# Mixing stage of a convolution and Laplace-operator kernel: a third output tile, weights one place sooner, POOL operations merged, sums evicted between the copies and run in pairs

## The chip, the cores and the metric

The kernel runs on one core of a Trainium2 chip. The metric is the device time of one execution in microseconds. A core has a matrix engine (PE, with its weight loads shown apart as PEld), a vector engine (DVE), an activation engine (ACT), a general engine (POOL), and a queue engine (SP) that here does nothing but issue DMAs. They work side by side and wait for each other through semaphores. PE writes its results into PSUM, eight banks per partition; ACT and DVE read them from there.

## The reference

Input is x of 16 images (b) with 16 channels and 256 x 256 points, fp32. There are two layers, each of the form x + layer(group-normalised x).

```python
# layer 0: circular 3x3 convolution
x = x + _L0_conv_ref(_gn(x), L0_conv_weight)
# layer 1: Laplace operator; alpha is the 2-D spectrum of gn(x)
alpha = jnp.fft.fft2(x, axes=(-2, -1))
A  = 1.0 / (omega1[:, None, None, None] - weights_pole1[None])
Bm = 1.0 / (omega2[:, None, None, None] - weights_pole2[None])
S  = jnp.einsum('ikpq,oikp,xikq->oxik', weights_residue, A, Bm)
output_residue1 = jnp.einsum('biox,oxik->bkox', alpha, S)
x1 = jnp.fft.ifft2(output_residue1, s=(Ny, Nx), axes=(-2, -1)).real
# residues, and exponentials exp(pole * t) of both directions
C = jnp.einsum('biox,oikp->bikpx', alpha, A)
D = jnp.einsum('bikpx,xikq->bikpq', C, Bm)
output_residue2 = jnp.einsum('bikpq,ikpq->bkpq', D, weights_residue)
E1 = jnp.exp(weights_pole1[..., None] * tyc)
E2 = jnp.exp(weights_pole2[..., None] * txc)
F  = jnp.einsum('kbpq,bipz->kbiqz', output_residue2, E1)
x2 = jnp.einsum('kbiqz,biqx->kizx', F, E2).real
x = x + (x1 + x2 / Nx / Ny)
```

What matters here are two lines: for every frequency (o, x) a 16 x 16 complex matrix `S` over channels (i, k) is formed, and the spectrum `alpha` of all images is multiplied by it (`output_residue1`). This is "mixing".

## The kernel before

The work runs in four stages, one after the other: the convolution with its norms (to about 600 us), the spectrum of the second layer (to about 1193 us), the mixing stage (to about 1863 us), and the inverse transform with the residue part and the output. In all but the mixing stage the change moves only a few loads and buffers.

The mixing stage is a loop over 32 *places* g, each of them four frequencies of one axis, and in each place over four *steps* n. A step does the following.

- `sums(n, w)`: 16 small matmuls (line 1032, two instructions each in the trace) multiply the weights `w` of the place by `ct` and so form a part of the matrices `S` of the next place g+1. They fill two banks `ps_s` out of a pool of four.
- `spread`: ACT (line 1049) and DVE (a stream shuffle, line 1052) copy these two banks into `sg` of the next place, twice each. Each engine begins with the other one's second bank: ACT reads bank 0 while DVE reads bank 1, and then they change over.
- `mix(m)`, four times: eight matmuls (line 1120, 16 instructions each in the trace) multiply `sg` of this place by the spectrum `abd` into a bank `ps_mix`, out of a pool of four. Each bank is then copied into the tile `yt` (line 1233), three by ACT and one by DVE, or two by each where ACT has other work in this step (`late`).
- `store`: four DMAs of 128 KB (line 1134) bring `yt` to the array `yD` in DRAM. `yt` has two buffers, one a step.
- `load`: up to four DMAs (line 1102 at n = 1, line 1107 at n = 2 and 3; nothing at n = 0) bring a part of the spectrum of the next place into `abd`.

All DMAs of stores and loads are issued on SP's queue, in the order of the program. Beside that run two generators, of which each step takes one piece. `weights(g + 2)` makes the weights that the sums of place g+1 use: three DVE operations at n = 0 (lines 903 to 910), a reciprocal and two more at n = 1 (lines 912 to 915), two at n = 2 (918 and 919), and then a POOL operation that spreads them into `w` (line 930; two buffers). `make_exps` makes the exponentials E1 and E2 in 16 rounds, of which each takes seven steps: POOL reduces the argument to the range of the sine (lines 1180 to 1195), ACT does Exp and Sin with a table load for each (1198 and 1201), POOL multiplies (1203 and 1205), and SP stores.

Nothing plans this order: `manual_schedule` keeps each engine's instructions in the order in which the program writes them, and each engine goes through its own in order. What a wait holds up is all that stands behind it on the same engine. Ahead of the loop `first_sums` makes the sums of the first place at once, and `finish_projections` (matmuls with `jmat`) finishes a part of the residues. At g = 30 and 31 `unmix_first` reads back, changes and writes again a part of the first place, on SP and DVE.

Of the kernel before, what the change touches and what calls it, by code (L numbers as in the profile page):

```python
# [9 lines left out]
FP = mybir.dt.float32  # L10
# [14 lines left out]
def conv_then_laplace_kernel(ctx: ExitStack, tc: tile.TileContext, a: dict, out: bass.AP):  # L25
# [28 lines left out]
    def const(name, shape):  # L54
        t = cp.tile(shape, FP, name=name, tag=name)
        later_loads.append((t, a[name]))
        return t

    cols = const("cols", [P, 24])
    kmask = const("kmask", [P, C])  # L60
    fold2 = const("fold2", [P, 2, 64])
    o2 = cp.tile([P, B, 2, 16], FP, name="o2", tag="o2")
    proj = cp.tile([P, 2, B, 16, 2], FP, name="proj", tag="proj")
    jmat = cp.tile([P, 3, P], FP, name="jmat", tag="jmat")
# [32 lines left out]
    tp = ptab.enter_context(tc.tile_pool(name="tables", bufs=1))  # L97
    vmr = tp.tile([P, 2, B, C], FP, name="vmr", tag="vmr")
# [59 lines left out]
    nc.sync.dma_start(out=jmat, in_=a["jmat"])  # L158
# [736 lines left out]
    def weights(g):  # L895
# [4 lines left out]
        u = up["u" if g else "u0"].tile([P, 4, 32, 4], FP, name="u", tag="u")  # L900
        w, den, e, f = (u[:, j] for j in range(4))
# [13 lines left out]
        nc.vector.scalar_tensor_tensor(f, w, nm0, pim, ALU.mult, ALU.add)  # L915
# [3 lines left out]
        nc.vector.tensor_tensor(v[:, :, 1], f, den, ALU.mult)  # L919
# [64 lines left out]
    yp = pool(p2, "yt", 2)  # L984
# [6 lines left out]
    zp = pool(p2, "between")  # L991
# [16 lines left out]
    zp.tile([P, 384], FP, name="between", tag="between")  # L1008
# [34 lines left out]
    def spread(n, *pairs):  # L1043


        for odd in range(2):
# [37 lines left out]

    def finish_projections():


        for ro in range(2):
            ps = pm.tile([P, B, 16], FP, name="ps_o", tag="ps_mix")
            nc.tensor.matmul(ps, lhsT=jmat[:, 0], rhs=accs[:, ro], start=True, stop=False)  # L1090
            nc.tensor.matmul(ps, lhsT=jmat[:, 2 - ro], rhs=accs[:, 1 - ro], start=False, stop=True)
            nc.vector.tensor_copy(o2[:, :, ro], ps)

# [67 lines left out]
    def make_exps(which):  # L1161
# [5 lines left out]
        nc.sync.dma_start(out=t, in_=a[("ty", "tx")[which]].to_broadcast([P, N]))  # L1167
        sign, phase, turns = (cols[:, 2 + 3 * which + j : 3 + 3 * which + j] for j in range(3))
# [4 lines left out]
        for q in range(8):  # L1173
            th = ep.tile([P, 2, N], FP, name="s_th", tag="s_th")
            rn = ep.tile([P, 2, N], FP, name="s_rn", tag="s_rn")
            tmp = ep.tile([P, 2, N], FP, name="s_tmp", tag="s_tmp")
# [4 lines left out]
            nc.gpsimd.tensor_scalar(rn, th, 1.0 / (2 * PI), turns, ALU.mult, ALU.add)  # L1181
            magic = 1.5 * 2.0**23
            nc.gpsimd.tensor_scalar(rn, rn, magic, None, ALU.add)
            nc.gpsimd.tensor_scalar(rn, rn, magic, None, ALU.subtract)
            yield
# [3 lines left out]
            for c in (c1, c2, c3):  # L1189
                nc.gpsimd.tensor_scalar(tmp, rn, float(c), None, ALU.mult)  # L1190
                nc.gpsimd.tensor_tensor(th, th, tmp, ALU.subtract)
                if c == c2:
                    yield
            nc.gpsimd.tensor_scalar(th, th, phase, 3.1415925, ALU.add, ALU.min)
            nc.gpsimd.tensor_scalar(th, th, -3.1415925, None, ALU.max)
# [5 lines left out]
            nc.scalar.activation(th, th, AF.Sin)  # L1201
# [17 lines left out]
    finish_projections()  # L1219
    unmix = None  # L1220
    exps, late = chain(make_exps(0), make_exps(1)), None
    for g in range(32):
        sg, w_now = ahead, wt
        steps = weights(g + 2) if g < 30 else iter(())
        ahead = new_sg(g + 1) if g < 31 else None
        for n in range(4):
            evict = sums(n, w_now) if ahead is not None else []
            yt = yp.tile([P, 2, 4 * B, 16], FP, name="yt", tag="yt")
            if evict:
                spread(n, (ahead, [z.rearrange("p q n -> p n q") for z in evict]))  # L1230
            for m in range(4):
                o, src = mix(4 * n + m, sg, yt)
# [6 lines left out]
            if n == 1 and unmix is not None:  # L1239
                next(unmix, None)  # L1240
            wt = next_step(steps, None) or wt
# [212 lines left out]
def _constants():  # L1454
# [47 lines left out]
    cols[:, 12:16] = p[:, None] // 8 % 4 == np.arange(4)  # L1502
    cols[:, 17] = p > 0
# [106 lines left out]
```

## Time and profile before

The kernel before takes 2619.7 us (median of three runs, 2618.83 to 2624.65). The profiled execution took 2623.94 us by itself; its span, from the first instruction to the last, is 2622.1 us.

| stretch (us) | length | PE | PEld | DVE | ACT | POOL | granted PE clock | DMA share | GB/s |
|---|---|---|---|---|---|---|---|---|---|
| span | 2622.1 | 2468.6 | 1885.3 | 1980.8 | 1432.6 | 1290.5 | 0.986 | | 249 |
| 1219 to 1862, mixing | 643 | 603.4 | 512.8 | 505.1 | 407.2 | 389.2 | 0.98 | 0.77 | 223 |
| 1874 to 2622, inverse and output | 748 | 729.2 | 641.1 | 509.3 | 306.1 | 412.0 | 0.99 | 0.82 | 281 |

The columns of the engines are busy time in microseconds. An engine counts as busy while an instruction of it runs; issuing DMAs and waiting don't count. The granted clock is the share of full speed that PE's clock was given, and the DMA share is the busy share of the 16 DMA engines. A line of a group names the line of the code, the engine, the operation, the tile written and the tiles read, the shape, the number of instructions, then busy time and the mean in ns, and then the idle time before them with what ended it. A line of the timeline gives start and length in microseconds, and in brackets the idle time ahead. A line of waits gives who waited, for whom, how long in all, how many times, and the longest.

### The profile page before, as it was taken

How to read it: one execution, taken by the hardware profiler on the slowest of the kernel's cores; microseconds unless marked ns; L12 is line 12 of the kernel's file. 1: busy time of each engine (PE TensorE's matmuls, PEld its weight loads, DVE VectorE, ACT ScalarE, POOL GpSimd, SP SyncE). 2: the span in 40 equal slices, each digit the busy share in tenths (PEclk: the TensorE clock that was granted, in tenths of full speed). 3: DMA queues.
4: the chain of work that ended last, by engine and by line, in shares of the span. 5: the costliest groups of instructions: out<-in, count | busy, mean ns of one | idle time of the engine just before them, and what ended most of it. 6: DMA issues, size and time to landing. Idle time of an engine off the chain costs nothing.

```text
span 2622.1 us, 84262 instructions
## 1 busy us (share of the span) xinstructions
PE 2468.6 (94%) x35314; PEld 1885.3 (72%) x35314; DVE 1980.8 (76%) x3772; ACT 1432.6 (55%) x2599; POOL 1290.5 (49%) x1179
## 2 busy tenths in 40 slices
PE   5998999989999999998999999999799999999998
PEld 2444455567777777775878778788688888888887
DVE  7777788848888888887877878887276676667666
ACT  2565566666666666665666656666244444444443
POOL 1333378433333333333666645766555565555553
PEclk9999999989999999999999999999899999999999
DMA  7888878854655655655777777777988888888884
GB/s 274 276 279 282 294 270 294 297 211 177 240 195 209 242 220 194 245 225 190 225 229 214 226 225 222 222 227 228 253 302 289 291 292 279 299 289 287 291 287 174
DMA packets 318011, 653.17 MB, mean 249 GB/s; under 512 B 49174, under 2 KB 163990, under 8 KB 305728
## 3 DMA queue, kind: packets, MB, share of 16 engines
q1 hardware_dynamic: 316464, 640.57, 72.4%
q8 instruction: 278, 4.55, 0.7%
q0 software_dynamic: 896, 3.02, 0.4%
q10 hardware_dynamic: 272, 4.19, 0.4%
q14 instruction: 101, 0.83, 0.1%
HBM read 368.15 MB, written 280.36 MB: 247 GB/s over the span
## 4 chain that ended last, share of the span: by engine, by line
PE 58%; DVE 7%; DMA 4%; SPq 3%; ACT 3%; POOL 2%; issue 1%; ACTq 0%; DVEq 0%; POOLq 0%
PE ps_mix L1120 9%; PE ps_y L777 9%; PE ps_y L785 8%; PE ps_p L1361 7%; PE ps_f L1385 7%; PE ps_f L1386 7%; PE ps_x L820 5%; DMA yD<-yt 4%; PE ps_s L1032 2%; SPq L1134 2%; PE ps_h L1345 2%; PE psd L805 1%; DVE r L1394 1%; DVE ol L1396 1%; DVE ol L1397 1%
## 5 line engine op out<-in xcount | busy, mean ns | idle before, releaser
L1120 PE MATMUL ps_mix<-abd,sg 128*64 128x128 f32 x8192 | 482.2, 276 | 39.4 <-DMA yD<-yt 16.6
L1120 PEld LDWEIGHTS ps_mix<-abd,sg 128*64 128x64 f32 x8192 | 451.9, 138 | 92.9 <-ACT yt L1233 55.7
L1325 POOL TENSOR_TENSOR u<-yk 128x512 f32<-128x512 f32 (+1 forms) x268 | 358.2, 1369 | 314.7 <-PE ps_p L1361 249.1
L305 PE MATMUL ps_conv<-xt,wc 32*32 32x512 f32 x12288 | 445.6, 602 | 36.0 <-issue 26.1
L305 PEld LDWEIGHTS ps_conv<-xt,wc 32*32 32x32 f32 x12288 | 251.1, 103 | 217.6 <-issue 127.0
L793 ACT ACTIVATE t<-ps_y,vmr 128x384 f32<-128x384 f32 x512 | 297.1, 580 | 161.1 <-PE ps_y L785 161.1
L1052 DVE STREAM_SHUFFLE sg<-ps_s 128x512 f32<-128x512 f32 (+1 forms) x264 | 329.1, 1316 | 0.0
L777 PE MATMUL ps_y<-tabE,vq 128*128 128x256 f32 x1024 | 313.2, 388 | 11.0 <-DVE vq L766 9.4
L785 PE MATMUL ps_y<-tabO,vq 128*128 128x256 f32 x1024 | 305.9, 380 | 0.0
L275 POOL TENSOR_TENSOR pair<-pair,far 128x1024 f32<-128x1024 f32 x64 | 151.7, 2370 | 304.1 <-DVE pair L272 207.7
L1385 PE MATMUL ps_f<-pt,inv 128*128 128x256 f32 x1008 | 300.4, 380 | 0.0
L1386 PE MATMUL ps_f<-hs,ey 128*128 128x256 f32 x1008 | 299.8, 379 | 0.0
L1361 PEld LDWEIGHTS ps_p<-inv,u 128*128 128x128 f32 x2048 | 268.9, 193 | 35.4 <-POOL u L1329 10.9
L1389 DVE TENSOR_TENSOR r<-ps_f,q 128x256 f32<-128x256 f32 x256 | 107.0, 418 | 241.9 <-ACT q L1388 241.9
L1361 PE MATMUL ps_p<-inv,u 128*128 128x128 f32 x2048 | 276.2, 278 | 9.8 <-POOL u L1329 9.7
L1049 ACT ACTIVATE sg<-ps_s,mcol 128x512 f32<-128x512 f32 (+1 forms) x264 | 179.3, 689 | 192.2 <-DVE sg L1052 117.1
L777 PEld LDWEIGHTS ps_y<-tabE,vq 128*128 128x128 f32 x1024 | 189.6, 191 | 87.5 <-ACT q L833 51.2
L1388 ACT COPY q<-ps_f 128x256 f32<-128x256 f32 x256 | 95.4, 373 | 274.7 <-PE ps_f L1386 250.4
L1363 ACT COPY pt<-ps_p 128x512 f32<-128x512 f32 x256 | 151.5, 592 | 134.9 <-PE ps_p L1361 134.9
L765 POOL TENSOR_TENSOR vq<-vf 128x512 f32<-128x512 f32 x64 | 81.4, 1272 | 291.6 <-DVE vf L769 281.5
L785 PEld LDWEIGHTS ps_y<-tabO,vq 128*128 128x128 f32 x1024 | 195.4, 191 | 26.9
L1233 ACT COPY yt<-ps_mix 128x512 f32<-128x512 f32 x352 | 184.1, 592 | 55.8 <-DMA yD<-yt 42.2
(237 smaller groups left out, 3993.6 us busy)
## 6 DMA issues: line engine op xcount, KB each, us to landing
xt<-in_x SPq DMA_DIRECT2D x288, 258.0 KB
vD<-pair SPq DMA_DIRECT2D x256, 256.0 KB
yD<-yt SPq DMA_DIRECT2D x512, 128.0 KB
vl<-vD SPq DMA_DIRECT2D x128, 512.0 KB
out_y<-ol SPq DMA_DIRECT2D x128, 512.0 KB
s<-vD SPq DMA_DIRECT2D x126, 512.0 KB
aD<-spec SPq DMA_DIRECT2D x15, 4096.0 KB
yk<-yD SPq DMA_DIRECT2D x60, 1024.0 KB
```

The lines of the kernel that those rows point to most:

```text
L305: nc.tensor.matmul(acc[r][32 * c : 32 * c + 32], lhsT=ready[b][0][rows, phase, tap], rhs=halves[b][u // 2][rows, q : q + 5 : 4, 2 - tap : ...
L777: nc.tensor.matmul(ps[:, 0:N], lhsT=vf[:, xo, 0, j], rhs=tabE[:, 0 : i + 2 : i + 1], start=True, stop=False, skip_group_check=True,)
L785: nc.tensor.matmul(ps[:, P : P + N], lhsT=vf[:, xo, 1, j], rhs=tabO[:, i : C + 1 : C - i], start=False, stop=True, skip_group_check=True,)
L793: nc.scalar.activation(t[:, xo, j].rearrange("p l n -> p (l n)"), ps[:, 0:384], AF.Copy, scale=vmr[:, 0, b0 + j, i : i + 1],)
L1049: nc.scalar.activation(to[..., k : k + 2], src[odd], AF.Copy, scale=nsgn)
L1052: nc.vector.stream_shuffle(to[..., C + k : C + k + 2], src[1 - odd], swap)
L1120: nc.tensor.matmul(ps[64 * t : 64 * t + 64, j], lhsT=sg[:, f : f + 2].rearrange("p f m -> p (f m)"), rhs=abd[jq][:, :, 2 * t + cc, 2 * jj ...
L1233: (nc.vector.tensor_copy if m >= (2 if late else 3) else nc.scalar.copy)(o, src)
L1325: nc.gpsimd.tensor_tensor(u[:, :, j].rearrange("p b (c n) -> p c b n", c=8), in0, in1, o)
L1361: nc.tensor.matmul(ps[:, at], lhsT=u[:, n], rhs=tab, start=True, stop=True)
L1385: nc.tensor.matmul(ps[:, e], lhsT=tab, rhs=pt[:, e], start=True, stop=False)
L1386: nc.tensor.matmul(ps[:, e], lhsT=ey[:, e], rhs=hs, start=False, stop=True)
```

## The change

- `yt` has three buffers in place of two.
- The sums of steps 0 and 1 are made in one run ahead of the mixing of step 0, and those of steps 2 and 3 ahead of the mixing of step 2; the mixing of two steps then runs without sums between. All four banks `ps_s` are filled by one run.
- `spread` is divided: its first half stands ahead of the first copy, its second half between the first copy and the second. ACT's order becomes activation, copy, activation, copy, copy, where both activations stood first before; DVE's order stays.
- The generator `weights` of a place begins at n = 3 of the place before, so that its pieces fall one step sooner; for the first one, its first piece stands ahead of the loop.
- In `make_exps` the two magic-number operations are one instruction, the phase is left to ACT's Sin as its bias, and the two clamps are one operation against two columns of constants. The rounding works on halves of 128 x 256, in an `rn` and a `tmp` of half the size.
- Room for the third buffer: `kmask` and `fold2` lie in a pool that is freed after the spectrum; `o2` takes the place of `proj`; `jmat` lies in a tile of the exponentials and is loaded after `ct`; the filler tile `between` is gone; `u` has three parts, as `f` is written over `w`.

```diff
@@ -51,17 +51,13 @@
     later_loads = []
-    def const(name, shape):
-        t = cp.tile(shape, FP, name=name, tag=name)
+    def const(name, shape, home=cp):
+        t = home.tile(shape, FP, name=name, tag=name)
         later_loads.append((t, a[name]))
         return t
     cols = const("cols", [P, 24])
-    kmask = const("kmask", [P, C])
-    fold2 = const("fold2", [P, 2, 64])
-    o2 = cp.tile([P, B, 2, 16], FP, name="o2", tag="o2")
     proj = cp.tile([P, 2, B, 16, 2], FP, name="proj", tag="proj")
-    jmat = cp.tile([P, 3, P], FP, name="jmat", tag="jmat")
     def pitched(name, rows, row, *split):
@@ -95,6 +91,8 @@
     ptab = ExitStack()
     tp = ptab.enter_context(tc.tile_pool(name="tables", bufs=1))
+    kmask = const("kmask", [P, C], tp)
+    fold2 = const("fold2", [P, 2, 64], tp)
     vmr = tp.tile([P, 2, B, C], FP, name="vmr", tag="vmr")
@@ -155,7 +153,6 @@
     own = m16[:, 0:C:2]
     load_consts()
     halves[1] = [load_x(1, h) for h in range(2)]
-    nc.sync.dma_start(out=jmat, in_=a["jmat"])
     ones = tp.tile([P, P], FP, name="ones", tag="ones")
     nc.vector.memset(ones, 1.0)
     tiny = wp.tile([P, 8], FP, name="tiny", tag="tiny")
@@ -897,8 +894,8 @@
         shape = [P, 32, 4]
-        u = up["u" if g else "u0"].tile([P, 4, 32, 4], FP, name="u", tag="u")
-        w, den, e, f = (u[:, j] for j in range(4))
+        u = up["u" if g else "u0"].tile([P, 3, 32, 4], FP, name="u", tag="u")
+        w, den, e = (u[:, j] for j in range(3))
         pr2, pre, pim = (prU[:, j].unsqueeze(2).to_broadcast(shape) for j in range(3))
         nc.vector.tensor_tensor(
             w,
@@ -912,11 +909,11 @@
         nc.vector.reciprocal(den, den)
         nc.vector.scalar_tensor_tensor(e, w, m1, pre, ALU.mult, ALU.add)
-        nc.vector.scalar_tensor_tensor(f, w, nm0, pim, ALU.mult, ALU.add)
+        nc.vector.scalar_tensor_tensor(w, w, nm0, pim, ALU.mult, ALU.add)
         yield
         v = up["v"].tile([P, 32, 2, 4], FP, name="v", tag="v")
         nc.vector.tensor_tensor(v[:, :, 0], e, den, ALU.mult)
-        nc.vector.tensor_tensor(v[:, :, 1], f, den, ALU.mult)
+        nc.vector.tensor_tensor(v[:, :, 1], w, den, ALU.mult)
         if g == 0:
             yield
         wt = wp.tile([P, 4, 8, 32], FP, name="w", tag="w")
@@ -981,14 +978,13 @@
     ptab.close()
-    yp = pool(p2, "yt", 2)
+    yp = pool(p2, "yt", 3)
     g0 = pool(p2, "sg0")
     a0 = pool(p2, "abd0")
     wp = pool(p2, "w", 2)
     ep = pool(p2, "exps")
     up["u"] = pool(p2, "u")
     a1 = pool(p2, "abd2")
-    zp = pool(p2, "between")
     tp = pool(p2, "ct")
     a2 = pool(p2, "abd3")
     g1 = pool(p2, "sg1")
@@ -1005,7 +1001,6 @@
         z.tile([P, 4, 4, 16, B], FP, name=f"abd{j}", tag=f"abd{j}") for j, z in ((2, a1), (3, a2))
     ]
-    zp.tile([P, 384], FP, name="between", tag="between")
     ct = tp.tile([P, 4, 8, N], FP, name="ct", tag="ct")
     nc.sync.dma_start(out=ct, in_=cD)
     def next_step(steps, w):
@@ -1040,10 +1035,10 @@
     swap = [p ^ 4 for p in range(32)]
-    def spread(n, *pairs):
-
-
-        for odd in range(2):
+    def spread(n, *pairs, odds=(0, 1)):
+
+
+        for odd in odds:
             for to, src in pairs:
                 k = 4 * n + 2 * odd
                 nc.scalar.activation(to[..., k : k + 2], src[odd], AF.Copy, scale=nsgn)
@@ -1082,14 +1077,19 @@
             load(0, jq)
         return sg, w1
+    jmat = ep.tile([P, 3, P], FP, name="jmat", tag="s_ex")
+    nc.sync.dma_start(out=jmat, in_=a["jmat"])
+
     def finish_projections():
+        o2 = cp.tile([P, B, 2, 16], FP, name="o2", tag="proj")
         for ro in range(2):
             ps = pm.tile([P, B, 16], FP, name="ps_o", tag="ps_mix")
             nc.tensor.matmul(ps, lhsT=jmat[:, 0], rhs=accs[:, ro], start=True, stop=False)
             nc.tensor.matmul(ps, lhsT=jmat[:, 2 - ro], rhs=accs[:, 1 - ro], start=False, stop=True)
             nc.vector.tensor_copy(o2[:, :, ro], ps)
+        return o2
     def load(g, jq, rows=range(4)):
@@ -1165,6 +1165,7 @@
         nc.sync.dma_start(out=pl, in_=a[f"pole_e{which + 1}"])
         t = ep.tile([P, N], FP, name="s_t", tag="s_t")
         nc.sync.dma_start(out=t, in_=a[("ty", "tx")[which]].to_broadcast([P, N]))
+        most, least = (cols[:, j : j + 1] for j in ((8, 10), (11, 18))[which])
         sign, phase, turns = (cols[:, 2 + 3 * which + j : 3 + 3 * which + j] for j in range(3))
         pim = ep.tile([P, C], FP, name="s_pim", tag="s_pim")
         for _ in range(4):
@@ -1172,33 +1173,31 @@
         nc.gpsimd.tensor_scalar(pim, pl[:, :, 1], sign, None, ALU.mult)
         for q in range(8):
             th = ep.tile([P, 2, N], FP, name="s_th", tag="s_th")
-            rn = ep.tile([P, 2, N], FP, name="s_rn", tag="s_rn")
-            tmp = ep.tile([P, 2, N], FP, name="s_tmp", tag="s_tmp")
+            rn = ep.tile([P, N], FP, name="s_rn", tag="s_rn")
+            tmp = ep.tile([P, N], FP, name="s_tmp", tag="s_tmp")
             ex = ep.tile([P, 2, N], FP, name="s_ex", tag="s_ex")
             for j in range(2):
                 i = 2 * q + j
                 nc.gpsimd.tensor_scalar(th[:, j], t, pim[:, i : i + 1], None, ALU.mult)
-            nc.gpsimd.tensor_scalar(rn, th, 1.0 / (2 * PI), turns, ALU.mult, ALU.add)
             magic = 1.5 * 2.0**23
-            nc.gpsimd.tensor_scalar(rn, rn, magic, None, ALU.add)
-            nc.gpsimd.tensor_scalar(rn, rn, magic, None, ALU.subtract)
-            yield
             c1 = 6.28125
             c2 = float(np.float32(1.93500518798828125e-3))
             c3 = 2 * np.pi - c1 - c2
-            for c in (c1, c2, c3):
-                nc.gpsimd.tensor_scalar(tmp, rn, float(c), None, ALU.mult)
-                nc.gpsimd.tensor_tensor(th, th, tmp, ALU.subtract)
-                if c == c2:
-                    yield
-            nc.gpsimd.tensor_scalar(th, th, phase, 3.1415925, ALU.add, ALU.min)
-            nc.gpsimd.tensor_scalar(th, th, -3.1415925, None, ALU.max)
+            for j in range(2):
+                z = th[:, j]
+                nc.gpsimd.tensor_scalar(rn, z, 1.0 / (2 * PI), turns, ALU.mult, ALU.add)
+                nc.gpsimd.tensor_scalar(rn, rn, magic, magic, ALU.add, ALU.subtract)
+                for c in (c1, c2, c3):
+                    nc.gpsimd.tensor_scalar(tmp, rn, float(c), None, ALU.mult)
+                    nc.gpsimd.tensor_tensor(z, z, tmp, ALU.subtract)
+                yield
+            nc.gpsimd.tensor_scalar(th, th, most, least, ALU.min, ALU.max)
             for j in range(2):
                 i = 2 * q + j
                 nc.scalar.activation(ex[:, j], t, AF.Exp, scale=pl[:, i, 0:1])
             yield True
             yield
-            nc.scalar.activation(th, th, AF.Sin)
+            nc.scalar.activation(th, th, AF.Sin, bias=phase)
             yield True
             nc.gpsimd.tensor_tensor(th, th, ex, ALU.mult)
             for op, eo in ((ALU.add, 0), (ALU.subtract, 1)):
@@ -1216,19 +1215,23 @@
     p2.enter_context(tc.manual_schedule())
     accs = yp.tile([P, 2, B, 16], FP, name="accs", tag="yt")
     ahead, wt = first_sums()
-    finish_projections()
+    o2 = finish_projections()
     unmix = None
     exps, late = chain(make_exps(0), make_exps(1)), None
     for g in range(32):
         sg, w_now = ahead, wt
-        steps = weights(g + 2) if g < 30 else iter(())
+        if g == 0:
+            steps = weights(2)
+            next(steps)
         ahead = new_sg(g + 1) if g < 31 else None
         for n in range(4):
-            evict = sums(n, w_now) if ahead is not None else []
+            if ahead is not None and n % 2 == 0:
+                banks = [sums(n + j, w_now) for j in range(2)]
+            evict = banks[n % 2] if ahead is not None else []
             yt = yp.tile([P, 2, 4 * B, 16], FP, name="yt", tag="yt")
-            if evict:
-                spread(n, (ahead, [z.rearrange("p q n -> p n q") for z in evict]))
             for m in range(4):
+                if evict and m < 2:
+                    spread(n, (ahead, [z.rearrange("p q n -> p n q") for z in evict]), odds=(m,))
                 o, src = mix(4 * n + m, sg, yt)
                 (nc.vector.tensor_copy if m >= (2 if late else 3) else nc.scalar.copy)(o, src)
             if n == 1 and g < 31:
@@ -1238,6 +1241,8 @@
                 load(g + 1, n, (2, 3) if n == 1 else range(4))
             if n == 1 and unmix is not None:
                 next(unmix, None)
+            if n == 3:
+                steps = weights(g + 3) if g < 29 else iter(())
             wt = next_step(steps, None) or wt
             late = g and next(exps, None)
         if g == 30:
@@ -1500,6 +1505,9 @@
     cols[:, 6], cols[:, 7] = np.where(even, np.pi / 2, 0), np.where(even, 0.25, 0)
     cols[:, 9] = np.where(even, -1.0, 0.0)
     cols[:, 12:16] = p[:, None] // 8 % 4 == np.arange(4)
+    for phase, most, least in ((3, 8, 10), (6, 11, 18)):
+        cols[:, most] = 3.1415925 - cols[:, phase]
+        cols[:, least] = -3.1415925 - cols[:, phase]
     cols[:, 17] = p > 0
     cols[:, 16] = -cols[:, 17]
     cols[:, 19] = np.where(p > 0, 1.0, 0.5)
```

## The prediction

> **What bounds the kernel now.** I read the totals by engine first, then the mixing stage alone (1219 to 1862 us, the only stage in which the order of the work changes), then its groups, its waits, and two stretches of it in order of time.
>
> ```profile
> PE 2468.6 (94%) x35314; PEld 1885.3 (72%) x35314; DVE 1980.8 (76%) x3772; ACT 1432.6 (55%) x2599; POOL 1290.5 (49%) x1179
> 1219.00:1862.00 643.00, 603.36 (x12200) 512.82 (x12192) 505.12 (x905) 407.15 (x681) 389.24 (x298) 0.98 0.77 223
> L1120 PE MATMUL ps_mix<-abd,sg 128*64 128x128 f32 x8192 | 482.2, 276 | 39.4 <-DMA yD<-yt 16.6 <-ACT yt L1233 13.8 <-ACT sg L1049 4.5
> L1032 PE MATMUL ps_s<-ct,w 64*32 64x256 f32 x3944 | 135.0, 382 | 0.1
> ```
>
> The second line lists, after the 643.00 us of the stretch, busy time of PE, PE's weight loads, DVE, ACT and POOL, then the granted clock, the share of the DMA engines and GB/s. PE is busy for 603 of 643 us: it leads, with some 40 us of idle time. The third line says where they lie: ahead of mixing matmuls, and put down to the landing of a store out of `yt`, to ACT's copies into `yt`, and only 4.5 us to `sg`. The sums (last line) wait for nothing. ACT's copies wait for the same landing:
>
> ```profile
> DVE yt L1233 <- PE ps_mix L1120: 69.1, 71, 5.7
> PEld ps_mix L1120 <- ACT yt L1233: 55.7, 67, 8.4
> ACT yt L1233 <- DMA yD<-yt: 42.2, 28, 10.3
> ```
>
> So the chain is: store lands, copy, PSUM bank free, matmul. Next a quiet stretch, then a place (one value of g) that starts late, as PE and SP have them:
>
> ```profile
> 1571.38 1.09 PE L1032 MATMUL ps_s<-ct,w 64*32 64x256 f32 x32
> 1572.40 3.71 PE L1120 MATMUL ps_mix<-abd,sg 128*64 128x128 f32 x64
> 1576.05 1.09 PE L1032 MATMUL ps_s<-ct,w 64*32 64x256 f32 x32
> ...
> 1410.73 1.23 SPq L1102 DMA_DIRECT2D abd<-aD  x2
> 1412.07 2.24 SPq L1134 DMA_DIRECT2D yD<-yt  x4
> 1413.12 1.56 ACT L1233 COPY yt<-ps_mix 128x512 f32<-128x512 f32 x3 [0.76 <-DMA yD<-yt]
> 1419.16 2.53 SPq L1107 DMA_DIRECT2D abd<-aD  x4
> 1419.88 3.71 PE L1120 MATMUL ps_mix<-abd,sg 128*64 128x128 f32 x64 [1.19 <-ACT sg L1049]
> 1421.80 2.97 SPq L1134 DMA_DIRECT2D yD<-yt  x4
> ```
>
> An undisturbed step is 1576.05 − 1571.38 = 4.67 us: sums 1.02, mixing 3.65. Four make a place of 18.68 us, and 32 places 597.8 us; the stage takes 643 (20.1 us a place). From the starts of PE's single matmuls, 31 of 124 steps took over 4.75 us, 37.5 us too long together, 31.8 of it at n = 0. The other 8 us are at the ends: the last place alone waits 8.2 us (1854.76) for a copy that waited 10.35 us for a store.
>
> SP is nearly as full as PE. It issues 934 DMAs in the stage, which take 615 us of its queue (a store 0.598 us in the mean, 0.448 median; a load 0.74 and 0.603), and it reaches a store 2.2 us (mean) after the copies are done.
>
> **Part 1: the third `yt` tile.** From the last copy of step n to the first copy of step n+2, which takes the same tile today, lie about 6.0 us (4.67 + 1.02 + 0.9 for the first mixing run − 0.6 for the copy). The tile is free after 2.2 (SP's lag) + 1.97 (four issues) + 2.6 (median landing after the issue; 4.0 for one in ten) = 6.8 us. So two tiles are just too few; with three there are 10.7 us against 6.8 to 8.2. Of PE's idle time 39.4 us, 30.4 (16.6 + 13.8) are of this kind. Gain: 30 to 33 us, if SP keeps up, and some of the 8.2 us at the end.
>
> **Part 2: sums of two steps in one run.** A mixing run after sums has 0.15 us of handing over and first weight load, sums have 0.14 of it, and eight sums take 0.216 us. One run of 64 is 1.889 us against 2 × 1.025, and one mixing run of 128 saves 0.15: 0.31 us a pair, two pairs a place, 31 places: −19.3 us of PE. A place becomes 18.05 us.
>
> What it adds is a wait. The two runs of sums of a place now take all four `ps_s` banks, where two lay idle before. With t = 0 at a place's start: the second run begins at 9.03, and its second half needs, at 9.92, the banks that the sums of step 1 filled. DVE frees them last: its copy of step 0 ends at 6.2, then come the reciprocal and two more operations of `weights` (1.65 us), then two shuffles (1.12 + 1.42 us), which end at 9.9 to 10.3. Queued behind the waiting sums are eight mixing groups, and ACT, DVE and the stores wait for those. The trace says 0.1 us of such waiting in the whole stage. The Trainium skill, PSUM — Partial Sum Buffer, "PSUM bank collisions raise a hardware error", has it that a bank is to be guarded against every other engine's access, readers against readers too; ACT's 117.1 us of waiting for DVE's shuffles is just that. By the row the pairing costs 0; by the rule the sums wait for the last reader, 0.1 to 0.4 us a place, 3 to 12 us. I take 0.25, hence 18.3 us a place.
>
> **Part 3: weights one place sooner.** The same DVE and POOL operations, one step earlier: three tensor_tensor at n = 3 (0.35 + 0.42 + 0.51), the reciprocal at n = 0, the last two and POOL's `w` at n = 1. `w` is then ready at about 12 us of a place and is wanted at 18. No DMA moves. 0 us, apart from what part 2 charged.
>
> **Part 4: spread split, ACT act/copy/act/copy/copy.** The second activation waits for DVE's first shuffle; the first copy no longer stands behind that wait, and frees its PSUM bank 0.6 to 1.4 us sooner. DVE's order stays. `sg` for the next place is complete at 17.65 and wanted at 19.9. 0 us; without that slack of 2.2 us each late microsecond would go to PE once a place.
>
> **Part 5: POOL.** The two magic-number operations become one, the phase goes into ACT's Sin, clamps become one: from the rows (926 × 2, 693, 1498, 1503, 3 × 1491, 3 × 1281, 2042, 1493, 1284, 2 × 731) 20.1 us for each of 16 rounds. The halves of 128x256 have no row of their own; between half of the 128x512 price and the same price they give 14 to 22 us, and I take 17.6 (the nearest row, the 926 ns of 128x256, lies between). POOL is busy 389 of 643 us and ahead of nobody on the path; hidden in every case. It meets DVE at the shared operations (the 910 line varies from 292 to 1410 ns), which is in the range of part 2.
>
> **Part 6: SBUF for the tile.** `between`, a quarter of `u` and half of `rn` and `tmp` go; `kmask` and `fold2` move. `jmat` is loaded after `ct` (192 KB, one DMA) once the spectrum's last tile is read near 1187 us, and is wanted at 1216: hidden by 29 us, and if not, all mixing starts later by the difference. ACT's first weights start some 3 us later, in front of a PE wait of 9.0 us (1204.59). 0 us.
>
> **The sum.** PE alone: 643 − 19.3 − 32 + 31 × 0.25 (7.8) = 599.5 us, and less at the end. SP: 615 us of issue holds some 40 in which the first store or load of a group waits for copies or matmuls, which a later SP no longer waits for, and some 70 in which an issue waits for one of the eight completion counters that the DMAs share. Base price 2.0 per four stores, 2.5 per four loads: 511 us. Bounds 575 to 615, I take 598 in the middle, and with 8 at the ends 606. The skill has a rule against this: DMA: Bandwidth & Descriptors, "Issuing engines are not separate DMA queues", says that the sequencer's time is usually small relative to the DMA itself. By it PE is the bound (599.5, −43 us). The row says 615 us of issue against 0.77 × 643 = 495 us of DMA engines: here issue is the larger. So by the row SP sets the pace, 606 us, −37. A tile more lets SP fall behind 3.9 us further, but PE would gain 0.2 us a step on it and have used that up in twenty steps. From the last place's 8.2 us I take no more than SP's own end allows, 0 to 5. Nothing outside the stage moves (the last 749 us start 10 us after its last store, as now). Profiled run 2623.94 (span 2622.1) − 37 = 2587; it lies 4.2 over the median of the runs, 2619.7, so the median becomes **2583 us**.
>
> **The rivals.**
> - *SP paces the stage* (likeliest, 0.45): 2583, from 2575 to 2597 with SP's bounds.
> - *PE paces it* (0.22): SP's counter waits shrink as stores spread over three tiles. 643 − 19.3 − 37.5 + 3 to 12 = 589 to 598: 2566 to 2575. For it: SP's store of 1.95 us for four at 1573; against it: 934 DMAs at the mean.
> - *The transfers push back* (0.18): more stores in flight make each issue wait longer for a counter. Other stages move 280 to 300 GB/s against 223, so there is room, but in 1 KB packets. With three quarters of the gain lost, 2600 to 2614, about 2607.
> - *Nothing of it arrives* (0.05): the late `sg` at n = 0 takes the place of the store's wait (its row has 4.5 us only): 2617 to 2623.
> - *Slower* (0.10): the `ps_s` banks. If POOL's many half-size operations slow DVE between copy and shuffle, the sums of step 3 stall in every place. The gain is gone at 37/31 = 1.2 us a place beyond the 0.25; at 2 us the kernel takes about 2645.
>
> **Chances and range.** Within 0.2% (5.2 us) a measurement can't tell the kernel from itself. Faster: 0.45 + 0.22 + nearly all of 0.18 = 0.84; same 0.06; slower 0.10. The range from 2565 to 2612 takes in the first two cases and most of the third.
>
> **What would show it.** Right: PE's waits for `yD<-yt` fall from 16.6 us to a few, mixing groups of 128 matmuls of 7.2 us, a place of 18.6 to 19.0 us, and SP without gaps. PE as the bound: places near 18.2, SP waiting for copies more than now. Wrong: rows of `ps_s` waiting for DVE or ACT `sg` of over 1 us at n = 1, a wait for `w`, or `yD<-yt` waits as large as before. If `jmat` is late, it shows ahead of 1218 us.

## The result and the profile after

The change makes no difference that can be measured. Over 14 runs of each kernel in turn on one chip the median is 2621.05 us with the change and 2622.41 us without; the ratio, taken over the runs and not from the two medians, is 1.0002, with a 95% interval from 0.999 to 1.0014. Forecast was 2583 us, in a range from 2565 to 2612.

The profiled execution of the changed kernel took 2615.02 us (span 2613.2). These are its lines that answer to those shown of before: the totals by engine, the mixing stage alone (length, busy time of PE, PEld, DVE, ACT, POOL, then clock, DMA share and GB/s), two groups and two waits. `sums` is now line 1027, the shuffle 1047, the copy 1236; mixing and stores keep lines 1120 and 1134.

```profile
PE 2458.4 (94%) x35314; PEld 1894.7 (73%) x35314; DVE 1971.9 (75%) x3772; ACT 1436.9 (55%) x2599; POOL 1259.3 (48%) x1275
...
1219.00:1862.00 643.00, 594.17 (x12132) 520.35 (x12128) 493.46 (x894) 410.58 (x681) 349.92 (x392) 0.98 0.77 225
...
L1120 PE MATMUL ps_mix<-abd,sg 128*64 128x128 f32 x8148 | 469.0, 276 | 34.3 <-DMA yD<-yt 24.0 <-DVE yt L1236 5.8 <-DMA abd<-aD 3.2
L1027 PE MATMUL ps_s<-ct,w 64*32 64x256 f32 x3904 | 126.5, 380 | 5.9 <-DVE sg L1047 3.7
...
ACT yt L1236 <- DMA yD<-yt: 27.8, 15, 3.5
PEld ps_s L1027 <- DVE sg L1047: 20.3, 30, 1.1
```

POOL is busy 39 us less, as worked out. A new wait of 20.3 us has come, of the sums for DVE's shuffles. And the idle time ahead of the mixing matmuls is there as before, 34.3 us, still put down mostly to stores out of `yt`, though `yt` has a third buffer. The prediction had named this as a sign of being wrong.

That name is wrong, in both profiles. Here is one late place of the changed kernel, SP's queue first and then PE:

```profile
1485.17 1.23 SPq L1102 DMA_DIRECT2D abd<-aD  x2
1486.51 2.77 SPq L1134 DMA_DIRECT2D yD<-yt  x4
1489.33 1.23 SPq L1102 DMA_DIRECT2D abd<-aD  x2
1490.67 2.74 SPq L1134 DMA_DIRECT2D yD<-yt  x4
...
1490.31 1.96 PE L1027 MATMUL ps_s<-ct,w 64*32 64x256 f32 x64
1494.60 8.83 PE L1120 MATMUL ps_mix<-abd,sg 128*64 128x128 f32 x128 [2.34 <-DMA yD<-yt]
```

The first mixing at 1494.60 reads `abd01`, whose last piece SP issued as the second DMA at 1489.33. The completion event of that DMA in the trace lies at 1494.46, 0.14 us ahead of the matmul. A DMA reports its landing on a completion counter, and SP's queue uses eight of them in turn (116 DMAs of this stretch on each). The matmul waits on the counters of the four loads into `abd01` and on PE's own semaphore; the store that the profile names was issued later, at 1491.24, on a counter that one of these loads had used. And one of the kernel before:

```profile
1492.62 3.04 SPq L1134 DMA_DIRECT2D yD<-yt  x4
1495.70 1.24 SPq L1102 DMA_DIRECT2D abd<-aD  x2
...
1499.93 3.71 PE L1120 MATMUL ps_mix<-abd,sg 128*64 128x128 f32 x64 [1.42 <-DMA yD<-yt]
```

Again the last piece of `abd01` lands 0.14 us ahead of the matmul. I compared the completion events of line 1102 with the first mixing in places 1 to 30. In the kernel before 21 places begin late, and in all 21 the last piece landed less than 0.5 us ahead; in the changed kernel it is 20 of 20 (in the second profiles, taken below, 17 of 19 and 22 of 22). The stores out of `yt` are another matter: in the kernel before the first copy of a step began within 0.25 us of their landing in 48 of 126 steps, in the changed one in 1 of 125, and at n = 0 never less than 2.6 us after it. So the third tile did free the copies, and PE waited at n = 0 for that load.

The rest is a sum over the stage. As a measure, called excess below, I take, from the starts of the sums, by how much the halves of a place exceed PE's own time: 9.03 us for a half in pairs, 4.67 us for a step without. "First" is the half with n = 0 and 1, where the place's first mixing lies; "second" the half with n = 2 and 3. The second half of the last place with sums is left out, since it runs into the stage's end.

| kernel | DMAs on SP | excess in first halves, us | in second halves | sum | ratio to before |
|---|---|---|---|---|---|
| before, two profiles | 920 | 31.8; 25.7 | 5.7; 7.7 | 37.5; 33.4, and 19.2 for unpaired sums: 56.7; 52.6 | 1 |
| changed, two profiles | 920 | 35.4; 38.1 | 15.9; 16.8 | 51.3; 54.9 | 1.0002 |

So PE gained 19.2 us by the pairs (0.62 us a place in 31 places) and lost nearly all of it in waits. DMAs are counted from the first store of the stage to the last.

### The profile page after: what moved, and what is told of

It is laid out like the page before. It is cut to its first block, busy times and chain, and to the rows that moved or that the text cites. A ratio compares the mean times of both kernels' runs of the same rounds, so it can differ in the third digit from the quotient of the medians.

```text
span 2613.2 us, 84265 instructions
## 1 busy us (share of the span) xinstructions
PE 2458.4 (94%) x35314; PEld 1894.7 (73%) x35314; DVE 1971.9 (75%) x3772; ACT 1436.9 (55%) x2599; POOL 1259.3 (48%) x1275
## 5 line engine op out<-in xcount | busy, mean ns | idle before, releaser
L1120 PE MATMUL ps_mix<-abd,sg 128*64 128x128 f32 x8192 | 471.4, 276 | 34.3 <-DMA yD<-yt 24.0
L1236 ACT COPY yt<-ps_mix 128x512 f32<-128x512 f32 x352 | 199.7, 583 | 139.0 <-issue 33.5
L1044 ACT ACTIVATE sg<-ps_s,mcol 128x512 f32<-128x512 f32 (+1 forms) x264 | 184.6, 699 | 96.2 <-DVE sg L1047 59.0
```

The source lines that it names most:

```text
L1044: nc.scalar.activation(to[..., k : k + 2], src[odd], AF.Copy, scale=nsgn)
L1120: nc.tensor.matmul(ps[64 * t : 64 * t + 64, j], lhsT=sg[:, f : f + 2].rearrange("p f m -> p (f m)"), rhs=abd[jq][:, :, 2 * t + cc, 2 * jj ...
L1236: (nc.vector.tensor_copy if m >= (2 if late else 3) else nc.scalar.copy)(o, src)
```

## The experiments

Theory A: SP's queue paces the stage, through the load into `abd01` (later split into A1, its issuing, and A2, the bytes that it moves). Theory B: the prediction's, copies wait for stores. Theory C: PE and the new wait for `ps_s` pace it. Theory D: the pairs gained, another part lost. All ratios are to the kernel before, run in turn on the same chip; the changed kernel equals it within 0.14%.

**Two tiles again (e1).**

```diff
-    yp = pool(p2, "yt", 3)
+    yp = pool(p2, "yt", 2)
```

> The changed kernel with two yt tiles in place of three, all else as changed. Theory A (the first mixing of a place waits for the last of the four loads into abd01, line 1102, which comes late on SP's queue): the third tile bought nothing on the path, so the time stays within 8 us of the changed kernel's 2621, and the landing of that load still comes 0.1 to 0.4 us ahead of the first mixing in most places. Theory B (the prediction's: the copies' wait for stores out of yt held PE up, and the third tile took that away, with its gain lost elsewhere): 25 to 33 us slower than the changed kernel, about 2650.

Measured: 2625.91 us, ratio 1.0029 (1.0017 to 1.0042), so some 8 us over the kernel before, and far from B's 25 to 33. The halves exceed by 23.9 and 29.2, in sum 53.1, the same as with three tiles. The 8 us aren't in the loop: with the smaller pool the load of `ct` is issued 0.1 us after the spectrum's last matmul, where it was issued 20 us ahead of it. First mixing starts 34.4 us after that matmul, against 29.2 and 26.7 us in the two profiles of the changed kernel.

```profile
PE ps_s L1027 <- DMA ct<-cD: 15.9, 1, 15.9
...
ACT yt L1236 <- DMA yD<-yt: 158.8, 77, 4.5
PEld ps_s L1027 <- DVE sg L1047: 28.8, 36, 1.5
PEld ps_s L1027 <- ACT sg L1044: 12.3, 16, 1.6
```

The other half of A's forecast failed. Only 5 of 30 places begin late, all 5 at the landing of the load, where it was to come last in most. The copies now wait for stores (second line, 27.8 us with three tiles), and begin within 0.25 us of a landing in 100 of 126 steps; behind them ACT and DVE are late with `ps_s`, and PE waits in its sums. Here B's wait does reach PE, at the same total. So the third tile changes what PE waits for, and not how long.

**Sums step by step (e2).**

```diff
-            if ahead is not None and n % 2 == 0:
-                banks = [sums(n + j, w_now) for j in range(2)]
-            evict = banks[n % 2] if ahead is not None else []
+            evict = sums(n, w_now) if ahead is not None else []
```

> The changed kernel with the sums of each step in a run of their own, as before; third tile, weights, spread and POOL as changed. Theory A (SP's queue paces the stage): PE's own place becomes 18.68 us instead of 18.05 plus 0.5 of waiting for the ps_s banks, and neither sets the pace: within 6 us of 2621. Theory C (PE paces it, and the pairs' 19 us are eaten by the 16 us of waiting for ps_s): 0 to 5 us slower, which is the same; but under C the wait ahead of the first mixing of a place would stay at 1.1 us in the mean, under A it shrinks by what PE's place grows, to about 1.0 us or less. Theory D (the pairs gained their 19 us and another part of the change lost them): 15 to 20 us slower, about 2640.

Measured: 2617.58 us, ratio 0.9999 (0.9985 to 1.0013). Excess 28.7 us at n = 0 (0.9 a place), none at all at n = 1, 2, 3. The 5.6 us that the kernel before had at n = 3 are gone; those were the part that stores out of `yt` did hold up: in six of its seven waits at n = 3 the copy that PE waited for had begun within 0.31 us of a store's landing. D falls. A and C both allow this time; the wait at n = 0 shrank as A has it.

**All four `abd01` loads ahead of the store (e3).**

```diff
-                load(g + 1, n, (0, 1))
+                load(g + 1, n)
             store(g, n, yt)
-            if g < 31:
-                load(g + 1, n, (2, 3) if n == 1 else range(4))
+            if g < 31 and n > 1:
+                load(g + 1, n)
```

> The changed kernel with all four loads into abd01 ahead of the store of step 1, where two of them stood behind it. Theory A: their landing comes some 2 us (four stores of 0.5 us) sooner against the queue, the wait of 1.1 us ahead of the first mixing of a place goes in most places, and the time falls by 15 to 35 us, to 2586 to 2606; less where SP has no slack to give (25 us of real waiting in the stage). Theory B: nothing, or slower, since the store of step 1 is issued 1.3 us later: 2621 or more.

Measured: 2618.17 us, ratio 1.001 (0.9997 to 1.0023): no gain, where A had 15 to 35 us. Excess 28.7 and 23.6, sum 52.3. The first halves lost a little waiting, the second halves took it. Moving one load forward in a full queue moves another DMA back; "SP has no slack to give" was the case.

**The last quarter's loads on ACT's queue (e4).**

```diff
-                nc.sync.dma_start(
+                queue.dma_start(
...
-            if g < 31:
+            if g < 31 and n < 3:
                 load(g + 1, n, (2, 3) if n == 1 else range(4))
+            if g and n < 2:
+                load(g, 3, (2 * n, 2 * n + 1), nc.scalar)
```

> The changed kernel with the four loads of the spectrum's last quarter (line 1107, n = 3) issued on ACT's queue, two after the copies of step 0 and two after those of step 1 of the next place, in place of SP's queue. Theory A: SP is rid of 124 issues of 0.66 us, 82 us in all, and paces nothing any more; the waits of 35 us ahead of the first mixings go, and ACT pays some 2.5 us a place out of its idle time: 2586 to 2602. Theories B and C: SP wasn't the bound, and ACT gets 80 us more: 2621 to 2640.

Measured: 2651.8 us, ratio 1.0131 (1.0105 to 1.0156), slower than all had it (B and C up to 2640), and not for their reason. SP waits for ACT's loads, which is new (waits on SP's own queue):

```profile
SPq L1134 <- DMA abd<-aD: 142.4, 61, 5.5
```

In this program SP and ACT draw their completion counters from one set of eight, in the order of the program. Where ACT is late with its DMA, SP's next DMA on that counter waits for it. The run doesn't decide on A.

**Without the last quarter's loads (e5), and with them on POOL's queue (e6, e7, e8).** e5 leaves work out, and its result is not the reference's. POOL has counters of its own.

```diff
-            if g < 31:
+            if g < 31 and n < 3:
                 load(g + 1, n, (2, 3) if n == 1 else range(4))
```

> The changed kernel without the loads of the spectrum's last quarter (line 1107 at n = 3, four DMAs in each of 31 places); the mixing of that quarter then works on the data of the first place, so that part of the output isn't the reference's. Theory A1 (SP's issue paces the stage: 920 DMAs at 0.64 us and 0.045 us between them): SP is rid of 124 x 0.66 = 82 us and is no bound any more, the waits ahead of the first mixing of a place (35 us) go, PE paces with 18.05 + 0.5 us a place: 2580 to 2592. Theory A2 (the DMA engines' traffic, 0.77 busy, makes loads land late): traffic falls by 16 of 144 MB, a ninth; 2600 to 2612. Theory C (PE and the ps_s wait): no change, 2615 to 2625.

Measured: 2572.23 us, ratio 0.982 (0.9796 to 0.9845), 8 us under the range of A1. All first halves but one are at 9.03 us; what is left are 16.0 us in the second halves, the wait for `ps_s`. PE, and then SP's waits:

```profile
1491.77 7.21 PE L1120 MATMUL ps_mix<-abd,sg 128*64 128x128 f32 x128
1498.90 1.09 PE L1027 MATMUL ps_s<-ct,w 64*32 64x256 f32 x32
1500.36 1.10 PE L1027 MATMUL ps_s<-ct,w 64*32 64x256 f32 x32 [0.36 <-DVE sg L1047]
1501.39 7.21 PE L1120 MATMUL ps_mix<-abd,sg 128*64 128x128 f32 x128
1508.52 1.96 PE L1027 MATMUL ps_s<-ct,w 64*32 64x256 f32 x64
1510.41 7.21 PE L1120 MATMUL ps_mix<-abd,sg 128*64 128x128 f32 x128
...
SPq L1134 <- DVE yt L1236: 66.4, 69, 2.0
```

SP now waits for copies, 66 us against 2.6 in the changed kernel: it has become the one that is early. Issue or bytes? The same bytes on POOL's queue (in e4's diff `nc.gpsimd` for `nc.scalar`):

> The changed kernel with the same four loads issued on POOL's queue, two after step 0 and two after step 1 of the next place: the same bytes, other queue and other completion counters than SP's. Theory A1: as without the loads, 2580 to 2596, POOL paying some 4 us a place out of 45% idle time. Theory A2: no change, 2615 to 2625. If POOL's issuing slows DVE or lands so late that the last quarter's mixing waits, 2625 to 2650.

> The kernel before, with these four loads on POOL's queue and nothing else changed: two yt tiles, sums step by step. Theory A1: the kernel before was paced by SP too and its waits at n = 0 (31.8 us) were for the load into abd01 and not for stores out of yt; PE alone would take 18.68 us a place: 2583 to 2596. Theory B (two yt tiles held it): at most 10 us faster, 2607 to 2620.

> As with the four loads on POOL's queue, and the weights at their old places (DVE's reciprocal and two more, 1.65 us, stand at n = 1 again and three tensor_tensor of 1.28 us at n = 0). If SP no longer paces, PE does, and its wait of 0.5 us a place for the ps_s banks of step 1 falls to 0.1 or 0.2: 9 to 12 us faster than with the weights moved. If something else still paces, no difference.

Measured: e6 2638.2 us (1.0069, 1.0049 to 1.0089), e7 2645.83 (1.0102, 1.008 to 1.0123), e8 2655.71 (1.0137, 1.0112 to 1.0162), all slower. e7 lies outside both of its ranges, and e8 is 17 us slower than e6 where 9 to 12 us faster was expected. With the same bytes, e6 has 0.1 us of excess in its first halves and 76.4 in the second; e7, the kernel before with its two tiles and the loads on POOL, 2.7 us at n = 0 in place of 31.8, and 64.9 at n = 3. That the waits at n = 0 go agrees with SP's queue as their cause. It doesn't show it alone, since SP gains time too in a place that the other waits make over 2 us longer; e9 and e17 decide. The loss is POOL's order: the loads stand behind the work for the exponentials and land when the last quarter's mixing already waits, as the third case of e6's expectation has it. This is e7's group:

```profile
L1120 PE MATMUL ps_mix<-abd,sg 128*64 128x128 f32 x8192 | 495.3, 281 | 53.2 <-DMA abd<-aD 27.3 <-issue 16.9 <-ACT yt L1233 5.7
```

**The loads at a better place of POOL's queue (e9 to e12).** They now stand where SP had them, at the end of step 3. e11 also has the weights at their old places; e12 leaves out the piece at n = 0 (last three lines), so that the reciprocal comes at n = 1. e8 had the weights as e11.

```diff
     def load(g, jq, rows=range(4)):
+        queue = nc.gpsimd if jq == 3 and g else nc.sync
...
-                nc.sync.dma_start(
+                queue.dma_start(
                     out=abd[jq][s::4, s].rearrange("r c j b -> r c (j b)"), in_=src[:, :, jq]
...
-            wt = next_step(steps, None) or wt
+            if n:
+                wt = next_step(steps, None) or wt
```

> The changed kernel with the loads of the last quarter on POOL's queue, at the place in the program where SP had them (end of step 3), ahead of POOL's work for the exponentials of that step; in the run with these loads in the next place they stood behind that work and landed up to 7 us late. Theory A1 (SP's issue paces; bytes don't matter): as without the loads, 2572 to 2588; first halves of a place at 9.03 us, second ones at 9.55. If bytes matter (A2), or POOL's own queue delays them again: above 2605, with second halves over 10 us.

> The kernel before, with these four loads on POOL's queue at the end of step 3. A1: its 31.8 us at n = 0 and most of the 5.6 us at n = 3 go: 2582 to 2595. B (two yt tiles hold it): 2607 or more. Against the changed kernel with the same loads on POOL, A1 has it at 0 to 8 us slower (PE's place 18.68 against 18.05 + 0.51).

> The changed kernel, the loads of the last quarter on POOL's queue at the end of step 3, and the weights at their old places. With PE pacing, the wait for the ps_s banks falls from 0.51 to 0.14 us a place: 10 to 12 us faster than with the weights moved. If SP or POOL still pace, no difference.

> As the one with the loads on POOL at the end of step 3, and the weights' first piece at n = 3 of the place before, none at n = 0, the reciprocal at n = 1, the last two at n = 2. DVE has nothing between the copy of step 0 and the shuffles of step 1, so the wait for ps_s goes wholly: second halves of 9.03 us, 14 to 16 us faster than with the weights moved as the change has them, 2 to 5 faster than with the weights at their old places. If DVE's work at n = 3 delays the shuffles of step 3, first halves grow instead.

Measured: e9 2599.96 us, ratio 0.994 (0.9922 to 0.9959), 16 us faster than the kernel before with the same bytes, so that these aren't the bound, though 12 us short of A1's range; e10 2624.77 (1.0034, 1.002 to 1.0048); e11 2619.69 (1.0018, 1.0008 to 1.0028); e12 2620.92 (1.0014, 1.0002 to 1.0027). These three miss what A1 and PE as the next bound had for them: e10 lies where B had it, though its wait at n = 0 falls from 31.8 to 8.7 us, and e11 and e12 are 20 us slower than e9 in place of 10 to 16 faster. In e9 the first halves exceed by 1.1 us, the second by 36.4: 16 of them the `ps_s` wait, most of the others POOL. The loads on POOL wait for PE (first line, e9), and behind them stands `w`. Where `w` is made a step later, as in e11, the sums wait for it (second line); e10 (22.7 us) and e12 (31.3 us) have the same row:

```profile
POOL abd L1108 <- PE ps_mix L1121: 52.1, 14, 7.3
...
PE ps_s L1027 <- POOL w L927: 32.5, 11, 4.4
```

So "weights one place sooner" buys room for a late POOL, and, as e14 shows next, puts the reciprocal where it makes the `ps_s` wait. In the change itself no row has the sums waiting for POOL's `w`.

**The `ps_s` wait taken away (e13, e14), and both kernels again (e15, e16).** The reciprocal goes behind the shuffles of step 1; `w` keeps its time.

```diff
                     spread(n, (ahead, [z.rearrange("p q n -> p n q") for z in evict]), odds=(m,))
+                    if n == 1 and m == 1:
+                        wt = next_step(steps, None) or wt
...
-            wt = next_step(steps, None) or wt
+            if n:
+                wt = next_step(steps, None) or wt
```

> The changed kernel with the loads of the last quarter on POOL's queue at the end of step 3 (as the run at 2600), and the reciprocal and its two operations behind the shuffles of step 1 in place of ahead of them; the last two and POOL's w keep their time. With PE pacing, the wait for ps_s of 0.51 us a place goes: second halves of 9.03 to 9.17 in most places, 10 to 16 us faster than 2600, so 2584 to 2591. If that wait was only the place where another bound showed, no gain: 2597 to 2603.

> The changed kernel with only that: the reciprocal and its two operations behind the shuffles of step 1. SP's queue as in the change. If SP paces (A1), the wait for ps_s goes and the first mixing of the next place waits longer by as much: 2617 to 2624, the same. If PE and this wait pace (C): 10 to 16 us faster, 2605 to 2611.

> The kernel before, unchanged, for a second profile. The stage from the first to the last mixing took 641.3 us in the first one, and the convolution ended at 565.3 us. If both are the kernel's own and not this execution's, the second profile has them within 1 us; if executions differ, the stage lies 3 us or more elsewhere, and the 10 us between the two kernels' stages are no measure of the change.

> The changed kernel, unchanged, for a second profile: stage 631.0 us and end of the convolution 558.1 us in the first one. By the medians of the two kernels (2621 and 2622) its stage should be nearer to 636 to 641 in a usual execution, by the profile 631.

e14 is the clearest of all: 2623.13 us, ratio 1.001 (0.9997 to 1.0024). The `ps_s` wait is gone, 4.3 us in the second halves for 15.9, and the first halves have 49.1 us for 35.4. The sum is 53.4, as in the change (51.3 and 54.9), in e1 (53.1) and in e3 (52.3). PE's waits moved, and SP's queue was the same. Second halves without a wait in the sums, and a first half that pays, in e14:

```profile
1446.07 1.96 PE L1027 MATMUL ps_s<-ct,w 64*32 64x256 f32 x64
1447.96 7.21 PE L1120 MATMUL ps_mix<-abd,sg 128*64 128x128 f32 x128
1455.10 1.96 PE L1027 MATMUL ps_s<-ct,w 64*32 64x256 f32 x64
1458.54 7.21 PE L1120 MATMUL ps_mix<-abd,sg 128*64 128x128 f32 x128 [1.48 <-DMA yD<-yt]
```

This speaks against C, which expected a gain of 10 to 16 us. e13 (0.9937, 0.9913 to 0.9961) is no faster than e9: excess 8.5 and 33.2, now POOL's `w` (9.5 us) and the last quarter's loads (11.0 us). The second profiles give the stage from the first to the last mixing 638.6 us (before) and 636.0 us (changed), against 641.3 and 631.0 in the first: executions of one kernel differ by 2.7 and 5.0 us, and by the second pair of profiles the stage is 2.6 us shorter with the change, where the first pair had 10.

**Half of these loads on POOL (e17, e18).** Two of four DMAs, after step 0, where PE is mostly through with the tile; e18 adds e14's edit.

```diff
-                load(g + 1, n, (2, 3) if n == 1 else range(4))
+                load(g + 1, n, (2, 3) if n % 2 else range(4))
+            if g and n == 0:
+                load(g, 3, (0, 1), nc.gpsimd)
```

> The changed kernel with two of the four last-quarter loads on POOL's queue after step 0 of the next place, where PE has long read the tile, and two left on SP. SP is rid of 62 x 0.66 = 41 us, about what the waits of the first halves amount to (35 us). If POOL's order was what kept the second halves long, they are 9.55 in most places: 2585 to 2600. If 41 us are too few for SP, first halves stay over 9.3 in the mean, 2600 to 2612. If POOL's loads land late again (a second half over 11 in many places): 2610 or more.

> As that, and the reciprocal and its two operations behind the shuffles of step 1. If PE then paces, another 8 to 12 us faster: 2575 to 2590. If SP paces again, nothing: the waits move from the second halves to the first, with the same sum.

Measured: e17 2591.22 us, ratio 0.9884 (0.9865 to 0.9903), the fastest version that computes all; e18 2592.91 (0.9893, 0.987 to 0.9915), no more. With 62 fewer DMAs on SP (858) and the same bytes, e17's halves exceed by 5.7 and 22.2, 16 of the latter being the `ps_s` wait. In e18 the sum rises to 32.7 for e17's 27.9: again the wait went elsewhere (12.9 in the first halves). What ends the last 10 us in either was not settled.

## Why the prediction was wrong

- **Part 1, the third tile: the step that failed.** "Of PE's idle time 39.4 us, 30.4 are of this kind" took the profile's names for causes. The waits at n = 0 were for `abd01`. What should have told me was in the working: 31.8 of 37.5 us lay at n = 0, while a wait for `yt` could come at any n. The arithmetic on the tile itself (6.0 us between the copies, 6.8 needed) was right, copies did wait in 48 steps; but four PSUM banks lay between them and PE, and only the 5.6 us at n = 3 reached PE. The sum has a slip too: the 13.8 us hold the 8.2 us of the last place, which were counted again at the end. I never asked what a first mixing reads.
- **The bound by SP: the right queue, the wrong size.** SP's queue paces, as the likeliest case had it, but at 598 us, 606 with the ends, and the stage took 631.0 and 636.0. From the first store to the last the kernel before issues 920 DMAs in 568.9 us; each is followed by 0.045 us before the next, 41 us in all, so SP is taken for 610 of the 637 us of that stretch. In the changed kernel it is 568.1 + 41 = 609 of 631 us. The 615 us of the working hold all of this; I took 17 off, as waits for copies and matmuls that a later SP no longer has. They stayed: between the issues and inside them such waits come, by my count, to 40 to 51 us in all four profiles. For nothing in the change takes a DMA off SP, and a late first mixing makes late copies, for which SP waits. e1, e3 and e14 show that the loop hands a wait on rather than lose it. Nor did issues wait for counters, to which I gave 70 us: in the changed kernel 134 issues took over 0.75 us, and ahead of each of them the DMA before it on its counter had landed. Some 70 us over the usual time of an issue remain, before and after, for which the profile names no cause.
- **Rule against row.** The Trainium skill (DMA: Bandwidth & Descriptors, "Issuing engines are not separate DMA queues") has issuing time as usually small beside the DMA; here the row was the better guide, and e17 shows it: the same bytes, 62 issues moved, 30 us less.
- **Part 2, the pairs.** 9.03 us a half, as worked out, and 0.51 us a place of waiting for `ps_s`, where the row had nothing, my working by the bank rule of the Trainium skill (PSUM — Partial Sum Buffer, "PSUM bank collisions raise a hardware error") had 0.1 to 0.4 and I took 0.25. The rule was the one to go by, and my size for it too small: it costs 16 us of the 19.2 that the pairs gain. While SP paces, neither counts: e2 and e14 change them without changing the time.
- **Parts 3 and 4.** Put at 0 us. No run took either out of the change alone, so that this is not shown; e11 and e12 show what the sooner weights are good for.
- **Part 5, POOL.** 389.2 to 349.9 us, 39 against the 40 worked out. It was put at no time, and no run took it out alone.
- **Part 6 and the ends, costed at 0.** Between the spectrum's last matmul and the first mixing lie 25.4 and 25.2 us before, 29.2 and 26.7 after (0.87 of it the longer first run of sums; in the profile with 29.2 the granted clock was 0.50 from 1210 to 1214 us, for 1.00 in the other, and PE's small matmuls there take 0.63 us for 0.38). Between the last mixing and the output's first matmul lie 12.9 and 12.0 us before, 17.8 and 17.3 after. There the loads of the last stage on POOL wait, as the new layout has it, for a store where they waited for a matmul (before, then changed):

```profile
POOL yk L1283 <- PE ps_mix L1120: 7.8, 1, 7.8
...
POOL yk L1288 <- DMA yD<-yt: 11.4, 1, 11.4
```

  That the moved tile is the cause was not tried alone. Over the whole way from the spectrum's last matmul to the output's first the means are 677.7 us (679.6; 675.7) and 679.1 us (678.0; 680.1): 6 us gained in the stage are given back at its ends. Outside that way the convolution ended at 565.3 and 564.0 us before and 558.1 and 559.1 after; in the other runs with the changed kernel's code for it, at any time between 556.6 and 567.5, so that this is no effect of the change.

The outcome is the rival "nothing of it arrives", which had a chance of 0.05, with another wait in the lead than the one it names: it had a late `sg`, and it was `abd01`.

## What to carry to other kernels

A wait for several semaphores is named after one of them. Before a change is built on the name, compare the landing of every operand with the start of the matmul, and ask whether the wait falls where the named cause could fall. Where a queue is nearly full, count its instructions with the time between them: here a change that took none off it gained nothing, whatever waits it removed, and a gain showed up as a wait elsewhere. Moving a part of a full queue to an engine with idle time is worth trying, at a place in its order where it has nothing to wait for: half of the last quarter's loads on POOL gave 1.2%, all of them gave from a gain of 0.6% to a loss of 1.4%.

## What the runs showed of the hardware

In these programs DMAs issued on SP and on ACT share eight completion counters, so that a late ACT holds up SP (142 us in e4); POOL's have eight others. Issuing a load of 128 KB took 0.55 us on POOL (median in e6) and 0.60 us on SP, which I had expected to differ more.
